# Scaled adjacency stored graph by graph, row of degrees in the raw adjacency's tile, and a new stage order in a two-layer graph network

## The chip, the cores and the metric

The kernel runs on one core of one Trainium2 chip. The time is the device time of one launch in microseconds (us). Several executions are timed and their median is compared; one more execution is profiled, and its span runs from the first to the last instruction. Engines are called TensorE (PE, with PEld for its weight loads), VectorE (DVE), ScalarE (ACT), GpSimd (POOL) and SyncE (SP, which issues nearly all DMAs here).

## The reference

There are 128 graphs of 128 nodes with 512 features each, all in float32, and one adjacency matrix of 128 x 128 per graph.

```
deg = sum(adj, axis=-1)
agg = (adj @ x) / max(deg, 1e-6)
x1  = layernorm(x + relu(concat(x, agg) @ W.T))          # W is 512 x 1024
h1  = relu(adj @ (x1 @ W1) + b1)
h2  = relu(adj @ (h1 @ W2) + b2)
out = layernorm(x1 + adj @ (h2 @ W3) + b3)
```

The kernel uses concat(x, agg) @ W.T = x @ Wa + (adj / deg) @ (x @ Wb), so that the first layer needs x times both halves of W, and then one product per graph with the scaled adjacency.

## The kernel before

**Work units.** The graphs are taken four at a time; the four are called a quad, and there are 32 quads. For each quad the code has 22 named stages: X (load transposed x and build sums of it), D (load the adjacency and compute the degrees), AT (load the transposed adjacency), L0 to L3 (x times both halves of W, called y and u), A0 and A1 (the aggregation: scaled adjacency times y, plus u, then relu, residual and layernorm; two graphs each), G0 to G3 (the products of x1 and the adjacency, one graph each), Ha and Hb (times W1), Sa and Sb (times W2), H2 (times the adjacency), Ta and Tb (times W3), Z0 and Z1 (the last product with the adjacency, layernorm, output).

**Products.** Products with weights use Winograd's form of Strassen's method, so seven block products stand for eight. This needs sums and differences of blocks, on the data (class `Data`) and on the weights (class `Weight`, `sums`, lines 346 to 354). A weight has seven places in its tile. `PLACE` (line 334) says which place each of the seven products reads: product 1 reads place 0, 5 reads 3, 6 reads 2, 2 reads 4, 7 reads 1, 4 reads 5 and 3 reads 6. In quads 0 and 1 the first layer uses one level of the method (line 599 is its matmul). From quad 2 on, most products use two levels (line 617 is the matmul), and the first layer's weights stream in from DRAM through six slots (`ring`, in the trace `ring<-forms` and `big<-forms`), one DMA per block.

**Degrees and scaled adjacency.** For quad q, `load_adj` brings the raw adjacency to the tile `ar`. `degrees` (line 550) reduces it on VectorE to `deg` (line 554), takes the maximum with a small number and the reciprocal (555, 556), writes the 128 x 4 result to DRAM (`dd`) and reads it back as one row of 512 numbers, the same in all 128 partitions, into the tile `ah`. `normalized` (called at the start of stage L0) multiplies the transposed adjacency `at` into `ah` in place. The tile `ah` has the shape [128, 128, 4]: the graph is the innermost index, as it is in the row. In A0 and A1 the matmul at line 916 takes `AH_T[:, :, g]` as its stationary operand. The matmul at line 1216 (Z0 and Z1) has the same shape, with `a[:, g, :]` of the tile `at`, whose shape is [128, 4, 128]. There are one `ar`, one `ah`, two `at`, two `deg` and two `dd`.

**Order.** Nothing is issued directly. The stages append operations, with estimated durations and with the keys that they read and write, to a plan (class `Plan`). The order in which stages advance is the written list `ORDER`: at step t, an entry "L0-3" advances stage L0 of quad t-3, if what `AFTER` asks for is done; otherwise the stage is put on a list and advances as soon as it can. `Plan.order` then simulates the engines with the estimates and picks, for each engine, the next operation. TensorE takes the first ready one of the next `AHEAD` (48) in the order; the other engines take the ready operation with the earliest due time, where due times follow from TensorE's order. `LEADS` are four lead times in us: an operation with a lead isn't started earlier than so long before it is due. The first is that of ScalarE's copies that seed a bank of PSUM, the second that of the loads of x for the residual, the third that of the inner sums, the fourth that of the streamed weights. The emitted program keeps this order on every engine, and SP issues its DMAs in it.

**Start.** The program begins with the loads of x of quad 0 and of the second half of W (`wb`), four blocks each, and with the sums of both. Loads of W1, W2 and W3 wait for the key "row of degrees".

Helpers record most operations, so many instructions bear one line: 327 is every two-operand instruction on VectorE, 329 those on GpSimd, 320 every DMA.

Of the kernel before, what the change touches and what calls it, by code (L numbers as in the profile page):

```python
# [11 lines left out]
OP = mybir.AluOpType  # L12
AX = mybir.AxisListType

P = 128
G = 4
# [19 lines left out]
class Plan:  # L36
# [5 lines left out]


    LAG = 0.15
    AHEAD, HELP, HOLD, SEEN, REST, SPARE = 48, 12.0, 5.0, 8, 25.0, 1
    DMA_US, DMA_RATE = 2.0, 0.22e6

    def __init__(self, pools):
# [176 lines left out]

BANKS = 8
SIZES = 9, 3, 6, 6
LEADS = 9.0, 6.0, 28.9, 943.1
AFTER = {
# [3 lines left out]
}  # L233
ORDER = """
    L2-4 Ta-6 L3-4 Ta-5 Tb-5 Ta-6 Z0-6 L0-3 L3-2 L1-4 Ta-6 Ha-4 L0-3 D L0-3 Sb-3 L1-4 AT-3 L1-3 Tb-6 Sa-4 L1-4 Sa-4
    H2-5 G2-3 L2-4 L2-4 Z0-3 Tb-6 Hb-5 Tb-5 G1-3 H2-5 Tb-6 L0-2 L0-3 Z1-6 X-2 Ha-3 L3-3 L1-3 Z0-5 A0-4 H2-5 G1-4 L3-3
    L3-4 H2-5 L3-3 L3-4 Sb-3 Ha-3 Ha-3 L2-3 Sb-4 Ta-5 Sa-3 G3-4 Tb-5 Tb-5 Sb-3 Hb-4 G2-4 X-1 AT-3 G0-2 Sb-4 L0-2 Ta-5
    A1-3 A1-4 A0-4 G3-4 L0-3 G0-3 H2-4 Sa-4 Sa-3 Z1-5 L1-3 D Sa-4 L0-2 Hb-2 Sa-2 Sb-2 Ha-3 A1-4 Z1-6 L1-3 L2-3 Sa-3
    Tb-5 Ta-5 L3-2 Ha-2 L2-2 L1-2 Sb-2 L2-3 A0-4 Ta-5 Sb-2 L2-3
"""  # L240


# [1 line left out]
def gnn_resnorm_kernel(  # L244
# [15 lines left out]
    nc = tc.nc  # L260
# [13 lines left out]
    def tile_of(shape, name):  # L274
        return sbuf.tile(shape, F32, tag=name, name=name)
# [7 lines left out]
    ROW_T = [tile_of([P, 4, 2, H], f"row{i}") for i in range(2)]  # L283
    U_T = [tile_of([P, 4, 2, H], f"u{i}") for i in range(2)]
    AR_T = tile_of([P, G, P], "ar")
    AT_T = [tile_of([P, G, P], f"at{i}") for i in range(2)]
    AH_T = tile_of([P, P, G], "ah")
    ND = 8
    DEG_T = [tile_of([P, G], f"deg{i}") for i in range(2)]
    DD_T = [dram.tile([P, G], F32, tag=f"dd{i}", name=f"dd{i}") for i in range(2)]  # L290
# [18 lines left out]
    def pinned(ins):  # L309
        return tc.keep_in_program_order(ins)  # L310

    def vector(n, emit, reads, writes, shared=False, lead=None):
        plan.op("DVE", 0.06 + 0.00123 * n, emit, reads, writes, shared, lead=lead)

    def scalar(n, emit, reads, writes, columns=0, lead=None):
        plan.op("ACT", 0.165 + 0.00083 * n + 0.1 * columns, emit, reads, writes, lead=lead)

    def dma(dst, src, reads, writes, size, queue="SP", lead=None):
        eng = nc.sync if queue == "SP" else nc.scalar
        plan.op(queue, 0.06, lambda: pinned(eng.dma_start(dst(), src())), reads, writes, size=size, lead=lead)  # L320

    def const(v):
        return lambda: v

    def add(eng, n, dst, a, b, reads, writes, op=OP.add, shared=False, lead=None):

        on_vector = lambda: pinned(nc.vector.tensor_tensor(dst(), a(), b(), op=op))  # L327
        if eng == "POOL":
            on_gpsimd = lambda: pinned(nc.gpsimd.tensor_tensor(dst(), a(), b(), op=op))  # L329
            plan.op("POOL", 0.03 + 0.00243 * n, on_gpsimd, reads, writes, True, other=(0.06 + 0.00123 * n, on_vector), lead=lead)  # L330
        else:
            vector(n, on_vector, reads, writes, shared)
# [5 lines left out]
    class Weight:  # L338
# [4 lines left out]
        def __init__(self, name, w, after=()):  # L343
            self.name, self.t, self.ti = name, W_T[name], WI_T.get(name)
            wv = w.rearrange("(h c p) (o n) -> p h o c n", p=P, c=2, o=2)
            for i, j, k in ((0, 0, 0), (0, 1, 3), (1, 1, 6), (1, 0, 4)):
                dma(const(self.t[:, k]), const(wv[:, i, j]), after, [(name, k)], P * 2 * H * 4)

        def sums(self):
            for d, a, b in ((1, 6, 3), (3, 3, 0), (2, 6, 3), (5, 4, 2)):  # L350
                add(
                    "DVE", F, const(self.t[:, d]), const(self.t[:, a]), const(self.t[:, b]),
                    [(self.name, a), (self.name, b)], [(self.name, d)], OP.subtract, True,
                )
# [68 lines left out]
    class Streamed:  # L423

        def parts(self, ps, i):
# [3 lines left out]
                lambda: RING_T[s.index][:, 0:n], const(FORMS[i - 1][:, ps[0] : ps[-1] + 1].rearrange("p k s n -> p k (s n)")),  # L429
                ["ring free"] + [("form", w, i, p) for w in range(2) for p in ps], [s], n * P * H * 4, lead=LEADS[3],  # L430
            )
            return [lambda j=j: RING_T[s.index][:, j] for j in range(n)], [s]

    class Data:
# [18 lines left out]
        def inner_sums(self):  # L453
            for ps in PAIRS:
# [13 lines left out]
                for dst, a, b, reads, writes, op in (  # L468
# [4 lines left out]
                ):  # L473
                    add("POOL", n * P, dst, a, b, reads, writes, op, lead=LEADS[2] if dst is first else None)

# [52 lines left out]
    def at(q):  # L528
        return AT_T[q % 2], [("at", q % 2)]

# [12 lines left out]
    def load_adj(q):  # L543
        dma(const(AR_T), const(adj[q]), (), ["ar"], P * F * 4)

# [4 lines left out]
    def degrees(q):  # L550
        d, kd = DEG_T[q % 2], [("deg", q % 2)]
        dd = DD_T[q % 2]
        queue = "ACT" if q == 0 else "SP"
        vector(512, lambda: pinned(nc.vector.tensor_reduce(d, AR_T, axis=AX.X, op=OP.add)), ["ar"], kd)
        vector(90, lambda: pinned(nc.vector.tensor_scalar(d, d, DEG_EPS, None, op0=OP.max)), kd, kd, True)
        vector(90, lambda: pinned(nc.vector.reciprocal(d, d)), kd, kd)
        dma(const(dd), const(d), kd, [("dd", q % 2)], 400000 if q else 800000, queue)
        dma(
            const(AH_T), const(bass.AP(tensor=dd.tensor, offset=dd.offset, ap=[[0, P], [G, P], [1, G]])),
            [("dd", q % 2)], ["ah", "row of degrees"], 400000, queue,  # L560
        )

    def normalized(q):
        t, k = at(q)
        ah = AH_T.rearrange("p i g -> p g i")
        add("DVE", 512, const(ah), const(t), const(ah), k + ["ah"], ["ah"], OP.mult, True)

    def bank_ap(s):
        return BANK[s.index]

    def quarters(p, n):
        return bank_ap(p).rearrange("p a (b n) -> p (a b) n", n=P)[:, 0:n]
# [50 lines left out]
    def v_part(v, n, g, c):  # L623
        return lambda: V_T[v.index][:, 0:n, g, c]
# [56 lines left out]
    def last_part(a, b, ps, joint, v, kv, sinks):  # L681
# [18 lines left out]

        scalar(n * P, lambda: pinned(nc.scalar.copy(quarters(pz, n), v_part(v, n, 1, 1)())), kv, [pz], lead=LEADS[0])
        add("POOL", n * P, v_part(v, n, 0, 1), v_part(v, n, 0, 1), v_part(v, n, 1, 1), kv, [(v, "d")], OP.subtract)
# [120 lines left out]
    def layernorm(i, ap, keys, of=None):  # L823

        i %= ND
        mv, rs = MV_T[i], RS_T[i]
        src, ksrc = of or (ap, keys)
        for j in range(2):
            st = ST_T[(2 * i + j) % ND]
            ks = [("st", (2 * i + j) % ND)]  # L830
            vector(512, lambda j=j, st=st: pinned(nc.vector.bn_stats(st, src(j))), ksrc(j), ks)
            vector(98, lambda j=j, st=st: pinned(nc.vector.bn_aggr(mv[:, j, :], st)), ks, [("mv", i, j)])
        kr, kb = factors(i, range(2))
        for j in range(2):
            r, b = rs[:, 0, j : j + 1], rs[:, 1, j : j + 1]
            scalar(
                512,
                lambda j=j, r=r, b=b: pinned(nc.scalar.activation(ap(j), src(j), AF.Identity, bias=b, scale=r)),
                kr + kb + ksrc(j), keys(j), columns=2,
            )  # L840
# [51 lines left out]
    def l0(q):  # L892
        return row(q, "y"), u_of(q)
# [13 lines left out]
    def seg_agg(q, m):  # L907
        y, u = l0(q)
        for g in (2 * m, 2 * m + 1):
            p, r = Slot("bank", seeded=True), Slot("s", spare=3)  # L910
            dma(lambda r=r: S_T[r.index].rearrange("p a b -> p (a b)"), const(x[q][:, g]), (), [r], P * F * 4, lead=LEADS[1])
            scalar(512, lambda g=g, p=p: pinned(nc.scalar.copy(bank_ap(p), u.graph(g))), u.keys((g,)), [p], lead=LEADS[0])
            plan.op(
                "PE", 0.858,
                lambda g=g, p=p: pinned(
                    nc.tensor.matmul(bank_ap(p), AH_T[:, :, g], y.graph(g), start=False, stop=True, skip_group_check=True)  # L916
                ),
                ["ah"] + y.keys((g,)), [p],
            )
            vector(  # L920
                512,
                lambda g=g, p=p, r=r: pinned(
                    nc.vector.scalar_tensor_tensor(
                        u.graph(g), bank_ap(p), 0.0, S_T[r.index], op0=OP.max, op1=OP.add
                    )
                ),
                [p, r], u.keys((g,)),
            )
            yield
        layernorm(4 * q + m, lambda j: u.graph(2 * m + j), lambda j: u.keys((2 * m + j,)))  # L930
# [194 lines left out]
    def seg_end(q):  # L1125
# [11 lines left out]
        def half(k):  # L1137
            return bank_ap(banks[k])[:, 0]

        for g, h in parts:  # L1140
            p, j = banks[g, h], g - 2
            scalar(
                256, lambda g=g, h=h: pinned(nc.scalar.copy(half((g, h)), u.graph(g)[:, h])), u.keys((g,)), [p], lead=LEADS[0]
            )
# [192 lines left out]
    for t in range(NG + max((lag for _, lag in tokens), default=0)):  # L1337
        for n, lag in tokens:
            q = t - lag
# [57 lines left out]
```

## Time and profile before

| What | Value |
|---|---|
| Median of 3 runs | 2249.04 us (2248.91 to 2249.4) |
| The profiled execution | 2250.41 us |
| Its span | 2248.5 us |
| TensorE matmuls busy | 2235.7 us, 99% of the span, 13624 instructions |
| TensorE weight loads busy | 1997.9 us, 89% |
| VectorE busy | 1534.5 us, 68% |
| ScalarE busy | 1330.8 us, 59% |
| GpSimd busy | 1168.4 us, 52% |
| DMA traffic | 333.14 MB, mean 148 GB/s |
| Granted clock of TensorE | 0.999 |

A line of the groups reads: line, engine, operation, output tile, inputs, shapes, count, then busy time and mean duration of one, then the idle time of that engine just before, with what ended it. Tiles are named without their number. In the timeline neighbouring instructions of one kind are merged, so a row has the start, the length and the count. A float32 matmul appears as two records, each with a weight load of its own. Ends of matmuls are modelled, so neighbouring matmuls overlap in the timeline; the distance from one start to the next is what counts.

### The profile page before, as it was taken

To read this page: it belongs to the slowest core of one execution; us is meant where nothing else is said; L and a number is where in the kernel's file an instruction comes from. 1 tells how busy PE (TensorE), PEld (TensorE's weight loads), DVE (VectorE), ACT (ScalarE), POOL (GpSimd) and SP (SyncE) were. 2 spreads that over 40 slices of the span, in tenths; PEclk is the share of its full clock that TensorE was granted. 3 is DMA by queue.
4 is the path that set the end of the run, shared out by engine and by line. 5 is a ranking of instruction groups with operands and counts; after the bars stand their busy time and mean duration, and the time that the engine had idled before them with its cause. 6 is when DMAs were issued, how large, how long until landed. Compare 5 with 4: busy or idle time off the path is not lost.

```text
span 2248.5 us, 39986 instructions
## 1 busy us (share of the span) xinstructions
PE 2235.7 (99%) x13624; PEld 1997.9 (89%) x13624; DVE 1534.5 (68%) x3384; ACT 1330.8 (59%) x2619; POOL 1168.4 (52%) x1508
## 2 busy tenths in 40 slices
PE   8999999999999999999999999999999999999998
PEld 7888889898898888998888989889898898888997
DVE  4766667666777667677666766667666777667674
ACT  2456656566565665566665656656566556665565
POOL 0245654556645465554565455654546655455540
PEclk9999999999999999999999999999999999999999
DMA  8453445534455444454444553445534455443431
GB/s 268 125 156 125 149 142 174 175 121 145 130 176 176 127 146 134 159 176 140 139 144 143 178 162 124 147 142 172 176 121 149 129 168 176 124 141 129 153 125 38
DMA packets 206330, 333.14 MB, mean 148 GB/s; under 512 B 27056, under 2 KB 72112, under 8 KB 206128
## 3 DMA queue, kind: packets, MB, share of 16 engines
q1 hardware_dynamic: 205696, 330.19, 46.1%
q8 instruction: 109, 1.79, 0.3%
q14 instruction: 93, 0.76, 0.1%
q10 hardware_dynamic: 432, 0.40, 0.1%
HBM read 290.46 MB, written 40.04 MB: 147 GB/s over the span
## 4 chain that ended last, share of the span: by engine, by line
PE 99%; DVE 0%; DMA 0%; issue 0%; SPq 0%; DVEq 0%; ACT 0%
PE bank L617 57%; PE bank L599 21%; PE bank L916 5%; PE bank L941 5%; PE bank L1029 5%; PE bank L1216 5%; DMA big<-in_w0T_dram 0%; DVE big L327 0%; PE bank L1148 0%; SPq L320 0%; DVE ah L327 0%; DVE end_st L1153 0%; DVEq L1392 0%; DVE bank L327 0%; DVE T L327 0%
## 5 line engine op out<-in xcount | busy, mean ns | idle before, releaser
L579 ACT COPY s<-bank 128x384 f32<-128x384 f32 (+1 forms) x567 | 306.6, 541 | 320.6 <-PE bank L617 172.3
L599 PE MATMUL bank<-T,w 128*128 128x256 f32 x1792 | 416.9, 379 | 0.0
L599 PEld LDWEIGHTS bank<-T,w 128*128 128x128 f32 x1792 | 333.5, 190 | 67.2 <-issue 28.7
L329 POOL TENSOR_TENSOR T<-T 128x512 f32<-128x512 f32 (+2 forms) x295 | 279.8, 971 | 199.6 <-DVE T L327 113.2
L327 DVE TENSOR_TENSOR v<-bank,s 128x512 f32<-128x512 f32 x240 | 164.3, 684 | 205.1 <-PE bank L617 204.3
L617 PE MATMUL bank<-big,ti 128*128 128x128 f32 (+1 forms) x1470 | 274.2, 320 | 0.0
L329 POOL TENSOR_TENSOR xT<-xT 128x512 f32<-128x512 f32 (+1 forms) x244 | 237.9, 975 | 36.0 <-DVE ti L327 23.6
L585 ACT COPY bank<-bank 128x512 f32<-128x512 f32 (+2 forms) x273 | 144.0, 527 | 180.0 <-PE bank L617 153.4
L617 PEld LDWEIGHTS bank<-big,ti 128*128 128x128 f32 x1470 | 218.4, 191 | 23.8 <-issue 4.3
L617 PEld LDWEIGHTS bank<-w,T 128*128 128x128 f32 x1680 | 218.3, 192 | 17.1 <-issue 7.2
L327 DVE TENSOR_TENSOR T<-T 128x512 f32<-128x512 f32 (+1 forms) x325 | 223.9, 713 | 8.8 <-ACT T L952 5.8
L617 PEld LDWEIGHTS bank<-w,ti 128*128 128x128 f32 x1680 | 216.1, 192 | 15.5 <-issue 7.2
L617 PE MATMUL bank<-w,T 128*128 128x128 f32 x1680 | 226.5, 275 | 0.0
L617 PE MATMUL bank<-w,ti 128*128 128x128 f32 x1680 | 226.5, 275 | 0.0
L617 PE MATMUL bank<-big,T 128*128 128x128 f32 x1680 | 226.4, 275 | 0.0
L617 PEld LDWEIGHTS bank<-big,T 128*128 128x128 f32 x1680 | 218.3, 192 | 7.7
L327 DVE TENSOR_TENSOR row<-bank,s 128x384 f32<-128x384 f32 (+2 forms) x254 | 119.0, 468 | 152.3 <-PE bank L617 124.8
L617 PE MATMUL bank<-ring,xT 128*128 128x256 f32 x840 | 216.7, 380 | 0.0
L617 PE MATMUL bank<-big,xT 128*128 128x256 f32 x840 | 216.7, 379 | 0.0
L329 POOL TENSOR_TENSOR v<-v 128x384 f32<-128x384 f32 (+1 forms) x61 | 69.3, 1136 | 278.9 <-DVE v L327 144.4
L327 DVE TENSOR_TENSOR v<-v 128x512 f32<-128x512 f32 (+1 forms) x299 | 190.7, 645 | 5.3 <-DVE T L327 0.3
L329 POOL TENSOR_TENSOR s<-s,v 128x256 f32<-128x256 f32 (+1 forms) x60 | 51.8, 863 | 255.2 <-ACT bank L1210 140.7
(99 smaller groups left out, 4166.1 us busy)
## 6 DMA issues: line engine op xcount, KB each, us to landing
big<-forms SPq DMA_DIRECT2D x315, 256.0 KB, 3.2
ring<-forms SPq DMA_DIRECT2D x315, 256.0 KB, 3.3
s<-in_x_dram SPq DMA_DIRECT2D x128, 256.0 KB, 5.9
out_dram<-s SPq DMA_DIRECT2D x126, 256.0 KB, 4.0
xT<-in_xT_dram SPq DMA_DIRECT2D x62, 512.0 KB, 5.6
big<-forms SPq DMA_DIRECT2D x105, 128.0 KB, 2.7
ring<-forms SPq DMA_DIRECT2D x105, 128.0 KB, 2.8
ar<-in_adj_dram SPq DMA_DIRECT2D x32, 256.0 KB, 2.6
```

The costliest lines, as they stand in the source:

```text
L327: on_vector = lambda: pinned(nc.vector.tensor_tensor(dst(), a(), b(), op=op))
L329: on_gpsimd = lambda: pinned(nc.gpsimd.tensor_tensor(dst(), a(), b(), op=op))
L579: scalar(n * P, lambda: pinned(nc.scalar.copy(quarters_of(s, n), quarters(p, n))), [p], [s])
L585: scalar(n * P, lambda: pinned(nc.scalar.copy(quarters(s, n), quarters(p, n))), [p], [s])
L599: nc.tensor.matmul(bank_ap(p)[:, o, :], lhsT, rhs, start=start and o == 0 and c == 0, stop=c == 1, skip_group_check=True,)
L617: nc.tensor.matmul(dst, ta(), tb(), start=start and n == 0, stop=True, skip_group_check=True)
L916: nc.tensor.matmul(bank_ap(p), AH_T[:, :, g], y.graph(g), start=False, stop=True, skip_group_check=True)
L941: nc.tensor.matmul(bank_ap(p)[:, c // 2, (c % 2) * P : (c % 2 + 1) * P], u.chunk(g, c), a[:, g, :], start=c == 0, stop=True, skip_group_ch ...
L1029: nc.tensor.matmul(bank_ap(p)[:, g // 2, (g % 2) * P : (g % 2 + 1) * P], s.chunk(g, o), a[:, g, :], start=g == 0, stop=True, skip_group_ch ...
L1216: nc.tensor.matmul(bank_ap(p), a[:, g, :], s.graph(g), start=False, stop=True, skip_group_check=True)
```

## The change

The row of degrees is read into the tile `ar` and not into `ah`. `normalized` multiplies `at` with that row, which it reads graph by graph with a step of four words, and writes the result to `ah`, which has now the shape [128, 4, 128]. The matmul of the aggregation takes `AH_T[:, g]`. `normalized` now reads the key "ar", so the next load of the adjacency comes after it.

In `Weight`, the raw block b01 is loaded to place 1 in all weights. Place 3 then gets b01 - b00, and place 1 is overwritten with b11 - b01; the seven final contents are the same as before, and so are the numbers of loads and of subtractions.

`AHEAD` goes from 48 to 32, `LEADS` and `ORDER` have new values.

```diff
-    AHEAD, HELP, HOLD, SEEN, REST, SPARE = 48, 12.0, 5.0, 8, 25.0, 1
+    AHEAD, HELP, HOLD, SEEN, REST, SPARE = 32, 12.0, 5.0, 8, 25.0, 1
...
-LEADS = 9.0, 6.0, 28.9, 943.1
+LEADS = 9.9, 5.6, 28.9, 902.9
...
 ORDER = """
-    L2-4 Ta-6 L3-4 Ta-5 Tb-5 Ta-6 Z0-6 L0-3 L3-2 L1-4 Ta-6 Ha-4 L0-3 D L0-3 Sb-3 L1-4 AT-3 L1-3 Tb-6 Sa-4 L1-4 Sa-4
...
+    Sa-4 L0-4 Sb-3 L2-4 Sb-4 Ta-6 L1-3 G2-2 Z1-5 Sa-5 Sb-5 L1-2 Tb-6 D Z1-7 A0-5 L0-2 Sa-5 A0-5 L0-2 Ha-1 G0-4 L2-2
...
+    ROW_OF_DEGREES = AR_T.rearrange("p g i -> p (g i)")
     AT_T = [tile_of([P, G, P], f"at{i}") for i in range(2)]
-    AH_T = tile_of([P, P, G], "ah")
+    AH_T = tile_of([P, G, P], "ah")
...
-            for i, j, k in ((0, 0, 0), (0, 1, 3), (1, 1, 6), (1, 0, 4)):
+            for i, j, k in ((0, 0, 0), (0, 1, 1), (1, 1, 6), (1, 0, 4)):
                 dma(const(self.t[:, k]), const(wv[:, i, j]), after, [(name, k)], P * 2 * H * 4)
 
         def sums(self):
-            for d, a, b in ((1, 6, 3), (3, 3, 0), (2, 6, 3), (5, 4, 2)):
+            for d, a, b in ((3, 1, 0), (1, 6, 1), (2, 6, 3), (5, 4, 2)):
...
         dma(
-            const(AH_T), const(bass.AP(tensor=dd.tensor, offset=dd.offset, ap=[[0, P], [G, P], [1, G]])),
-            [("dd", q % 2)], ["ah", "row of degrees"], 400000, queue,
+            const(ROW_OF_DEGREES), const(bass.AP(tensor=dd.tensor, offset=dd.offset, ap=[[0, P], [1, G * P]])),
+            [("dd", q % 2)], ["ar", "row of degrees"], 400000, queue,
         )
 
     def normalized(q):
         t, k = at(q)
-        ah = AH_T.rearrange("p i g -> p g i")
-        add("DVE", 512, const(ah), const(t), const(ah), k + ["ah"], ["ah"], OP.mult, True)
+        r = ROW_OF_DEGREES.rearrange("p (i g) -> p g i", g=G)
+        add("DVE", 512, const(AH_T), const(t), const(r), k + ["ar"], ["ah"], OP.mult, True)
...
-                    nc.tensor.matmul(bank_ap(p), AH_T[:, :, g], y.graph(g), start=False, stop=True, skip_group_check=True)
+                    nc.tensor.matmul(bank_ap(p), AH_T[:, g], y.graph(g), start=False, stop=True, skip_group_check=True)
```

More of the change, by code (lines that the diff above doesn't have):

```diff
@@ L234 @@
 ORDER = """
-    L2-4 Ta-6 L3-4 Ta-5 Tb-5 Ta-6 Z0-6 L0-3 L3-2 L1-4 Ta-6 Ha-4 L0-3 D L0-3 Sb-3 L1-4 AT-3 L1-3 Tb-6 Sa-4 L1-4 Sa-4
[L236 to L239, printed above, removed]
+    Sa-4 L0-4 Sb-3 L2-4 Sb-4 Ta-6 L1-3 G2-2 Z1-5 Sa-5 Sb-5 L1-2 Tb-6 D Z1-7 A0-5 L0-2 Sa-5 A0-5 L0-2 Ha-1 G0-4 L2-2
+    L0-2 Ta-4 Tb-5 L3 G3-2 Ha-1 L3-3 L0 Sb-1 Tb-5 A0-3 Sb-1 L2-4 Ta-6 Sb-3 Ta-6 L1-4 X Hb-2 Ha-2 L1-2 L3-4 H2-3 A1-4
+    Hb-5 Tb-6 Sa-3 H2-5 L2-3 L2-4 L2-4 Ha Sa-3 D-2 Tb-4 L0-2 Sb-2 A1-1 Sa-1 L1-4 H2-4 Z1-6 Sa-3 L2-2 L3-1 L0-3 L3-1
+    Tb-5 L1-4 L1-4 L3-3 Ha-2 L2-4 L0-3 H2-5 L3-4 Ta-5 L3-4 Hb-3 G0-3 Sa-1 Tb-5 Ta-5 G3-4 G1-2 AT-3 L1-3 AT-2 G1-1 Ta-4
+    Z0-3 Tb-3 A1-4 G2 Ha-1 Z0-4 Ta-5 X H2-3 Sb-2 Z0-1
 """
```

## The prediction

> **What bounds the kernel now.** I read the waits of TensorE first, then the groups of instructions, then TensorE's timeline at the lines that the change touches, then the queue of SP. The waits of TensorE, whole (engine, line, what it waited for: total us, times, longest):
>
> ```profile
> PE bank L599 <- DMA big<-in_w0T_dram: 5.5, 1, 5.5
> PE bank L599 <- DVE T L327: 0.8, 1, 0.8
> PE bank L916 <- DVE ah L327: 0.2, 1, 0.2
> ```
>
> Three waits, 6.5 us of 2248.5, all in the first 90 us. The chain that ended last repeats itself with the quads (start, length):
>
> ```profile
> 755.26 21.75 PE bank L617 x148
> ...
> 824.65 21.75 PE bank L617 x148
> ```
>
> So a quad costs 824.65 - 755.26 = 69.39 us, TensorE never waits in it, and whatever VectorE, ScalarE or a DMA gains there is worth nothing. Only the pace of TensorE's own instructions counts. The groups show one kind that is out of line (busy us, mean ns of one | idle before):
>
> ```profile
> L916 PE MATMUL bank<-row,ah 128*128 128x512 f32 x256 | 128.2, 622 | 0.2 <-DVE ah L327 0.2
> L1216 PE MATMUL bank<-row,at 128*128 128x512 f32 x252 | 123.4, 592 | 0.0
> L916 PEld LDWEIGHTS bank<-row,ah 128*128 128x128 f32 x256 | 74.2, 314 | 15.7 <-DVE ah L327 0.6
> L1216 PEld LDWEIGHTS bank<-row,at 128*128 128x128 f32 x252 | 47.7, 190 | 20.1 <-issue 15.3
> L327 DVE TENSOR_TENSOR ah<-at,ah 128x512 f32<-128x512 f32 x32 | 38.1, 1189 | 39.3 <-DMA at<-in_adjT_dram 39.3
> ```
>
> L916 and L1216 have the same shape and the same moving operand (a graph of a row tile). They differ in the stationary one: `at` is stored graph by graph, 128 neighbouring words per graph; `ah` has the graph innermost, so a graph's weights lie 16 bytes apart. Its weight load takes 314 ns against 190, its matmul 622 ns against 592. The timeline says when that costs TensorE time (start, length; an f32 matmul is two records):
>
> ```profile
> 794.42 1.06 PE L617 MATMUL bank<-big,ti 128*128 128x128 f32 x8
> 795.31 1.14 PE L916 MATMUL bank<-row,ah 128*128 128x512 f32 x2
> 796.29 0.83 PE L617 MATMUL bank<-w,T 128*128 128x128 f32 x6
> ```
>
> The next matmul starts 0.98 us after L916's pair. The first run of L916 in the same quad has three graphs, from 790.83 to 793.53: 2.70 us. A pair of L1216 entered behind a matmul of the same short kind (128 columns) takes 0.86:
>
> ```profile
> 2221.99 1.02 PE L1216 MATMUL bank<-row,at 128*128 128x512 f32 x2
> 2222.85 1.95 PE L1029 MATMUL bank<-at,row 128*128 128x128 f32 x16
> ```
>
> So 0.98 - 0.86 = 0.12 us, and 2.70 - 3 x 0.86 = 0.12 us: it is lost once per run, at its entry, where the matmul in front gives only 0.11 us of cover (8 of them take 0.89 us) for a 0.31 us load. Two runs a quad: 0.24 us of the 69.39.
>
> [...] inside a run the 0.31 us load hides behind a 0.43 us matmul and nothing is lost. [...] The scaling of `ah`, source and destination both at 16-byte steps, takes 1189/512 = 2.3 ns[...]; a contiguous form is in the trace at 713 ns (line 327, T<-T).
>
> **The change part by part.**
>
> *Weights of the aggregation.* `ah` becomes graph by graph, so L916's load is then what L1216's is: 190 ns, and the entry costs nothing. From the groups: (622 - 592) x 256 = 7.7 us; from the quads: 2 x 0.12 x 32 = 7.7 us. **-7.7 us**, on the path. From the other side, if a run entered behind 128 columns still lost a part, down to 0; L1216's pair above, 0.86 with exactly that entry, makes me take the full value.
>
> *The scaling.* 32 instructions, now with one hopping source and a contiguous destination. Between 1189 ns as now and 713 ns[...]. Worth 0: TensorE doesn't wait for it. It starts at 753.62 in the quad above, its first user at 790.83, 36 us after its end; only in the second quad (0.2 us of wait) is that cover gone.
>
> *Row of degrees into `ar`.* Same DMA, 2 KB to each partition, same number. It no longer waits for the aggregation of the quad before to let go of `ah`; it waits for the reduction and the write of the degrees. In return the load of the next adjacency waits until the scaling has read `ar`. Then follow adjacency (2.6 us to land), reduction 0.68, two small ones 0.16 + 0.18, write of the degrees 1.6, row about 3.3: 8.5 us, where the next scaling is 69 us away. Worth 0.
>
> *b01 loaded to its own place.* Four loads and four subtractions per weight as before, so 0 for w1, w2, w3 and the second half of w0, which lie behind TensorE's work. Only the first weight is in the open:
>
> ```profile
> 6.91 2.14 DVE L327 TENSOR_TENSOR big<-big 128x512 f32<-128x512 f32 x3 [6.04 <-DMA big<-in_w0T_dram]
> 8.97 0.42 DVE L327 TENSOR_TENSOR ti<-big 128x256 f32<-128x256 f32 x1
> 9.31 0.68 DVE L327 TENSOR_TENSOR T<-T 128x512 f32<-128x512 f32 x1
> ```
>
> VectorE began when the third block (b11) had landed, since b01 lay where the difference of b01 and b00 must go. Now that difference needs b00 and b01 alone and starts one load earlier, 0.7 us. But TensorE's second product, at 10.05, waits for the sum of T at 9.31, whose last block lands at about 8.9. So at most 0.4 us of the 0.7 come through: **-0.3 us** (between 0 and -0.4; TensorE's first matmuls run at half pace there, 0.43 us instead of 0.22).
>
> *Order, lead times, window of 32.* Instructions on TensorE stay the same in kind and number. Read stage by stage, the new order has the same cycle per quad, with small exchanges among aggregation, second aggregation and layer 3, and the same end for the last quad. What it can still gain is small: the pauses other than those above are about 0.4 us at 86.8 us (the second quad's scaling) and 0.3 us at 2185. Taken as 0, from -0.7; above, no row excludes a loss, which is the second rival.
>
> **Sum.** -7.7 - 0.3 = -8.0 us. Against the profiled execution: span 2248.5 to 2240.5, its time 2250.41 to 2242.4. The median shown is 1.37 us below that execution's time: 2249.04 - 8.0 = **2241.0 us**. A quad goes from 69.39 to 69.15.
>
> **Rivals.** *The entry stall stays.* Should its cause be not the stride but the several waits of L916 (bank seeded by ScalarE, row, `ah`), only the start is gained: 2249.04 - 0.3 = 2248.7. Against it: L1216 waits for a seeded bank too and loses nothing.
>
> *A new wait in each quad, slower.* The three DMAs of the degrees now come right after the scaling, which runs when the streamed weights of the joint product start to flow on the same queue. SP issues in order, so while one of them waits for VectorE, streamed loads stand behind it. Six slots of 4 x 0.216 = 0.86 us each give 5.2 us from release to reuse; a load takes 3.2 to 3.3 us to land; cover 1.9 us. A hold of h costs h - 1.9 each in 30 quads. It eats the gain at h = 1.9 + 8.0/30 = 2.2 us, and is slower by over 0.2% from 2.3 us. At 2.7 us: 2241 + 24 = 2265. For it: the queue has had longer holds (total, times, longest):
>
> ```profile
> SPq L320 <- PE bank L916: 117.1, 36, 6.4
> SPq L320 <- DVE deg L554: 100.0, 28, 3.9
> SPq L320 <- DMA ah<-dd: 80.4, 28, 3.5
> ```
>
> Against it: these are the very waits that the change removes or shortens (row behind L916, adjacency behind the reduction, write behind the row's landing), and none reached TensorE. The new one, behind the scaling, is planned at 0.69 us[...].
>
> *Part of the gain lost.* Seeding banks 0.9 us earlier holds banks longer; a pause of 0.1 to 0.2 us per quad would give 2244 to 2247.
>
> **Chances.** Forecast 0.80; part lost 0.07, half of it still past the limit; entry stall stays 0.05; slower 0.08. A difference of 0.2%, 4.5 us, is about what can be told from none. Faster 0.83, same 0.09, slower 0.08. The forecast's own range is 2239 to 2243.5 (start and order at their best, or some 2 us of scattered pauses); the range for 8 in 10 reaches into the partial loss: 2238.5 to 2246.5.
>
> **What would show it.** Right: L916's load at 190 ns and matmul at 592; pairs of L916 0.86 us apart at each entry; a quad of 69.15 us; no wait of TensorE beyond the start; the scaling below 1.1 us; SP no longer waiting for DVE deg L554. Wrong: a wait of TensorE for streamed loads, banks or `ah` in every quad, or the entry still at 0.98.

## The result: 0.35% slower

The changed kernel takes 2258.27 us (median of 7 runs, 2254.73 to 2260.54), the kernel before 2249.29 us on the same chip: ratio 1.0035, 95% interval 1.0026 to 1.0044. The prediction was 2241.0 us, faster. The profiled execution has a span of 2256.4 us against 2248.5.

The aggregation did what was forecast. From the groups of the changed kernel (line numbers are one higher than before; busy us, mean ns of one | idle before):

```profile
L917 PE MATMUL bank<-row,ah 128*128 128x512 f32 x256 | 125.4, 593 | 0.0
L917 PEld LDWEIGHTS bank<-row,ah 128*128 128x128 f32 x256 | 41.5, 191 | 16.5 <-ACT bank L913 9.6 <-issue 6.7
L328 DVE TENSOR_TENSOR ah<-at,ar 128x512 f32<-128x512 f32 x32 | 35.8, 1119 | 3.2 <-DMA at<-in_adjT_dram 3.2
```

The weight load went from 314 to 191 ns, the matmul from 622 to 593. The scaling is hardly faster, 1119 ns after 1189. But TensorE's waits have two new lines, for streamed weights:

```profile
PE bank L600 <- DMA big<-in_w0T_dram: 5.1, 1, 5.1
PE bank L618 <- DMA ring<-forms: 3.1, 4, 1.0
PE bank L618 <- DMA big<-forms: 2.4, 2, 1.6
```

The chain that ended last shows one of them (start, length):

```profile
1521.58 22.07 PE bank L618 x146
...
1591.17 22.08 PE bank L618 x146
...
1620.63 5.25 DMA ring<-forms
...
1661.91 22.08 PE bank L618 x146
```

The first of these two quads takes 69.59 us, the one with the DMA on the chain 70.74; before it was 69.39, predicted 69.15. So there is a loss in every quad, and a larger one in some. The first kind is not in the list of waits. It shows in the timeline of TensorE, at the matmuls of stage H2 (L1030), and beside them VectorE's:

```profile
1543.49 1.05 PE L1030 MATMUL bank<-at,row 128*128 128x128 f32 x8
1544.38 0.83 PE L618 MATMUL bank<-w,ti 128*128 128x128 f32 x6
1545.06 2.94 PE L1030 MATMUL bank<-at,row 128*128 128x128 f32 x24
1547.83 0.38 PE L618 MATMUL bank<-big,ti 128*128 128x256 f32 x1
```

```profile
1545.33 0.56 DVE L328 TENSOR_TENSOR row<-bank,s 128x384 f32<-128x384 f32 x1 [1.56 <-PE bank L618]
```

Eight records take 0.89 us from start to start, so 24 should take 2.67; they take 2.77. The product `w,ti` begins at 1544.38, VectorE sums its result into the row from 1545.33 to 1545.89, and the second of the three H2 groups, due at 1545.95, reads that row. There is one group of 0.89 us between, and the way over VectorE takes a little longer.

To count all such losses I took the distance between the starts of neighbouring matmuls, less the usual one of their kind (0.112 us for 128 columns, 0.216 for 256, 0.429 for 512), wherever more than 0.015 us was left. "Pauses" below means this, between 130 and 2150 us of the span, so in the steady part:

| Pauses, us | before | after |
|---|---|---|
| Entry of the aggregation | 7.0 | 0 |
| Streamed joint products, over 0.15 us each | 0 | 6.7 |
| Streamed joint products, up to 0.15 us each | 0.0 | 7.4 |
| H2 (L1030) | 0 | 2.7 |
| Z (L1217) | 0 | 1.6 |
| Sum | 7.0 | 18.3 |

The steady part lost 11.3 us. Before 130 us the pauses and half-pace matmuls fell from 5.7 to 2.1, after 2150 us they rose by 0.4. Together +8.1 us, and the span grew by 7.9.

### The profile page after: what moved, and what is told of

Its sections match the earlier page's. It is cut to its first block, busy times and chain, and to the rows that moved or that the text cites. A ratio compares the mean times of both kernels' runs of the same rounds, so it can differ in the third digit from the quotient of the medians.

```text
span 2256.4 us, 39844 instructions
## 1 busy us (share of the span) xinstructions
PE 2238.9 (99%) x13624; PEld 1963.4 (87%) x13624; DVE 1524.8 (68%) x3376; ACT 1331.4 (59%) x2619; POOL 1227.9 (54%) x1516
## 3 DMA queue, kind: packets, MB, share of 16 engines
q8 instruction: 109, 1.79, 0.3%
## 4 chain that ended last, share of the span: by engine, by line
PE 98%; DMA 1%; ACT 0%; DVE 0%; issue 0%; DVEq 0%; SPq 0%; ACTq 0%
PE bank L618 56%; PE bank L600 22%; PE bank L1030 5%; PE bank L942 5%; PE bank L917 5%; PE bank L1217 5%; DMA ring<-forms 1%; DMA big<-forms 0%; DMA big<-in_w0T_dram 0%; PE bank L1149 0%; DVE end_st L1154 0%; DVEq L1393 0%; ACT u L839 0%; ACT T L953 0%; ACT bank L586 0%
## 5 line engine op out<-in xcount | busy, mean ns | idle before, releaser
L580 ACT COPY s<-bank 128x384 f32<-128x384 f32 (+1 forms) x567 | 304.6, 537 | 291.8 <-PE bank L618 200.7
L600 PE MATMUL bank<-T,w 128*128 128x256 f32 x1792 | 407.3, 379 | 0.0
L330 POOL TENSOR_TENSOR T<-T 128x512 f32<-128x512 f32 (+1 forms) x243 | 231.8, 969 | 171.3 <-PE bank L600 59.8
L618 PE MATMUL bank<-big,ti 128*128 128x128 f32 (+1 forms) x1512 | 282.3, 321 | 0.0
L328 DVE TENSOR_TENSOR T<-T 128x512 f32<-128x512 f32 (+1 forms) x377 | 215.2, 591 | 70.9 <-ACT T L966 38.9
L618 PEld LDWEIGHTS bank<-big,ti 128*128 128x128 f32 x1512 | 227.2, 191 | 28.2 <-issue 14.9
L328 DVE TENSOR_TENSOR v<-v 128x512 f32<-128x512 f32 (+1 forms) x301 | 222.4, 747 | 1.4 <-DVE rstd L328 0.4
L618 PE MATMUL bank<-ring,xT 128*128 128x256 f32 x852 | 222.2, 383 | 0.0
L1227 DVE SCALAR_TENSOR_TENSOR s<-bank,u 128x512 f32<-128x512 f32 x124 | 85.4, 689 | 201.8 <-PE bank L1217 201.7
L330 POOL TENSOR_TENSOR ti<-T 128x256 f32<-128x256 f32 (+1 forms) x149 | 90.7, 617 | 197.9 <-DVE ti L328 197.9
```

What stands on the lines that cost most here:

```text
L580: scalar(n * P, lambda: pinned(nc.scalar.copy(quarters_of(s, n), quarters(p, n))), [p], [s])
L600: nc.tensor.matmul(bank_ap(p)[:, o, :], lhsT, rhs, start=start and o == 0 and c == 0, stop=c == 1, skip_group_check=True,)
L618: nc.tensor.matmul(dst, ta(), tb(), start=start and n == 0, stop=True, skip_group_check=True)
L1227: nc.vector.scalar_tensor_tensor(S_T[o.index], bank_ap(p), 1.0, u.graph(g), op0=OP.mult, op1=OP.add, accum_out=total)
```

## The experiments

The ratios are against the kernel before, timed beside each run (medians of 2249.29 to 2251.23 us), so a difference between the medians of two experiments is uncertain by 1 or 2 us.

**The layout alone.** The order of all engines is that of the kernel before:

```diff
-    AH_T = tile_of([P, P, G], "ah")
+    AH_T = tile_of([P, G, P], "ah")
+    ROW_OF_DEGREES = tile_of([P, G, P], "rowd").rearrange("p g i -> p (g i)")
...
-        ah = AH_T.rearrange("p i g -> p g i")
-        add("DVE", 512, const(ah), const(t), const(ah), k + ["ah"], ["ah"], OP.mult, True)
+        r = ROW_OF_DEGREES.rearrange("p (i g) -> p g i", g=G)
+        add("DVE", 512, const(AH_T), const(t), const(r), k + ["ah"], ["ah"], OP.mult, True)
...
```

> The kernel before, with the order of every engine untouched; only the scaled adjacency is stored graph by graph, and the row of degrees is read into a tile of its own, from which the scaling reads it. Theory (the layout takes the entry stall of the aggregation away, and it is the new order that lost time): L916's weight load 190 ns, no 0.12 us at the entry of its runs, a quad of 69.15 us, 2249.3 - 7.7 = 2241.6 us. Rival (the layout itself brings a wait elsewhere, through the slower or earlier scaling): 2249 us or more.

Measured: 2243.46 us, ratio 0.997 (0.9959 to 0.9982). TensorE's waits are those of the kernel before, and the chain gives a quad of 820.00 - 750.86 = 69.14 us:

```profile
PE bank L599 <- DMA big<-in_w0T_dram: 5.5, 1, 5.5
PE bank L599 <- DVE T L327: 1.0, 1, 1.0
PE bank L916 <- DVE ah L327: 0.2, 1, 0.2
```

```profile
750.86 21.75 PE bank L617 x148
...
820.00 21.75 PE bank L617 x148
```

Pauses in the steady part fell from 7.0 to 0.4 us. The layout wins 0.3%, as forecast; the loss comes from elsewhere.

**The order without the layout.** The changed kernel with the old storage of `ah`:

```diff
-    AH_T = tile_of([P, G, P], "ah")
+    AH_T = tile_of([P, P, G], "ah")
...
-        add("DVE", 512, const(AH_T), const(t), const(r), k + ["ar"], ["ah"], OP.mult, True)
+        add("DVE", 512, const(AH_T.rearrange("p i g -> p g i")), const(t), const(r), k + ["ar"], ["ah"], OP.mult, True)
...
```

> The changed kernel, with the order of every engine untouched; only the scaled adjacency has the graph as its innermost index again. Theory (layout and order are independent, the order costs some 16 us and the layout wins 7.7): 2258 + 7.7 = 2266 us, the entry stall of 0.12 us back in each run of the aggregation. Rival (with the other waits there, the entry stall is hidden behind them): 2258 us as the changed kernel.

Measured: 2268.80 us, ratio 1.0085 (1.0071 to 1.0099). That is 10.5 us above the changed kernel (11 by the ratios), not 7.7. The pauses at the entry of the aggregation are back with 10.6 us in 87 events, three in a quad where the kernel before had two: the new order splits the four matmuls into three runs. The entry stall is there with either order, and without the new layout the rest of the change costs 0.85%.

**b01 at its own place, alone.** The two lines of `Weight` in the kernel before:

```diff
-            for i, j, k in ((0, 0, 0), (0, 1, 3), (1, 1, 6), (1, 0, 4)):
+            for i, j, k in ((0, 0, 0), (0, 1, 1), (1, 1, 6), (1, 0, 4)):
...
-            for d, a, b in ((1, 6, 3), (3, 3, 0), (2, 6, 3), (5, 4, 2)):
+            for d, a, b in ((3, 1, 0), (1, 6, 1), (2, 6, 3), (5, 4, 2)):
```

> The kernel before, with b01 loaded to its own place and the sums in the new sequence, and the old order list (the planned order differs a little, mostly in the first quads). Theory: the start gains what the two profiles differ by in the first product of TensorE, up to 3 us of pauses and half-pace matmuls, so 2246.5 to 2249 us. Rival (the start gains nothing, since its pace was set by the landing of x and by when TensorE reaches full pace): 2249 us.

Measured: 2247.71 us, ratio 0.9988 (0.9981 to 0.9994), so 2.7 us. VectorE's timeline at the start shows why it is more than the 0.3 of the prediction:

```profile
6.44 0.69 DVE L327 TENSOR_TENSOR T<-T 128x512 f32<-128x512 f32 x1 [5.57 <-DMA T<-in_xT_dram]
7.66 2.09 DVE L327 TENSOR_TENSOR big<-big 128x512 f32<-128x512 f32 x2 [0.53 <-DMA big<-in_w0T_dram]
```

The sum of T, before at 9.31, stands now in front. Since the second product no longer needs b11, the planner gives that load a later due time and issues x first. TensorE's second product starts at 9.07 us and not at 10.05. The rest lies in the half-pace matmuls: their 33rd starts at 14.36 us and not at 17.23. How much of that is luck can't be told from single profiles, since the layout alone, with the start of the kernel before, has it at 15.36.

**Both data parts, old order list.** The edits of the first and the third experiment together.

> The kernel before with its old order list, the scaled adjacency graph by graph with the row of degrees in a tile of its own, and b01 loaded to its own place: both parts of the change that touch data, without the new order, the new lead times and the window of 32. Theory (the three parts add up): 7.7 us from the layout and 2.7 from the start, 2250.4 - 10.4 = 2240 us, faster than both kernels; so the new order alone costs some 18 us. Rival (the parts overlap at the start, or the order of before has no room either): 2243 us as the layout alone.

Measured: 2240.54 us, ratio 0.9953 (0.994 to 0.9967): the parts add up, and this is faster than both kernels. Steady pauses are 1.2 us. What the changed kernel has besides (the shared tile, the order, the lead times, the window) therefore costs 1.0035 / 0.9953 = 1.0082, some 18 us. No run takes the order list, the lead times and the window apart.

**The x loads made small.** The changed kernel with

```diff
-dma(lambda r=r: S_T[r.index].rearrange("p a b -> p (a b)"), const(x[q][:, g]), ...
+dma(lambda r=r: S_T[r.index].rearrange("p a b -> p (a b)")[:, 0 : 512 if q < 4 else 64], const(x[q][:, g, 0 : 512 if q < 4 else 64]), ...
```

> The changed kernel, with the order of every engine untouched; from quad 4 on the loads of x for the residual carry 64 of the 512 features (the other 448 columns of the residual are left out, the slot keeps what it held). The same number of DMAs stands in the queue. Theory (the streamed weights come late because the burst of x loads shares the DMA engines with them): no wait of TensorE for streamed loads, the 6.7 us of pauses over 0.15 us in the middle gone, 2258 - 7 = 2251 us; small pauses of 0.05 to 0.09 us stay where they are not at streamed loads. Rival (SP holds them back, or their slots come free too late): 2258 us, the waits unchanged.

Measured: 2252.89 us, ratio 1.0012 (1.0005 to 1.0018), 5.4 us below the changed kernel. TensorE's waits for streamed weights fell from 5.5 us to 0.9:

```profile
PE bank L618 <- DVE u L328: 0.8, 1, 0.8
PE bank L618 <- DMA ring<-forms: 0.7, 1, 0.7
PE bank L600 <- DVE big L328: 0.2, 1, 0.2
PE bank L618 <- DMA big<-forms: 0.2, 1, 0.2
```

Pauses over 0.15 us fell from 6.7 to 2.4; the small ones hardly moved (6.5 at joint products, 2.6 at H2, 1.6 at Z). The burst is in SP's timeline of the changed kernel, around the load that stood on the chain:

```profile
1618.04 0.32 SPq L321 DMA_DIRECT2D ring<-forms  x1
1618.47 1.66 SPq L321 DMA_DIRECT2D big<-forms  x3
1620.63 0.32 SPq L321 DMA_DIRECT2D ring<-forms  x1
1621.00 0.90 SPq L321 DMA_DIRECT2D s<-in_x_dram  x2
1621.94 0.90 SPq L321 DMA_DIRECT2D ring<-forms  x2
```

The landing times grow within this burst, from 2.06 us for its first load to 8.00 for its last x load, issued at 1623.85. The streamed load issued at 1620.63 took 5.25 us to land, where the median is 3.5.

To see how much time a load has in hand, each one was matched with the product that reads its place, by the slots of the plan. The last six streamed loads of a quad land 1.2 to 3.6 us before their use in the kernel before (medians by place), and 0.2 to 1.25 us before it in the changed one, 0.13 at the least, as with the load on the chain: it landed at 1625.89 and TensorE, which waited for it, began at 1626.02. The kernel before has a burst of the same kind, but it comes later in the quad:

```profile
784.06 0.32 SPq L320 DMA_DIRECT2D big<-forms  x1
784.50 0.36 SPq L320 DMA_DIRECT2D ring<-forms  x1
784.91 0.90 SPq L320 DMA_DIRECT2D s<-in_x_dram  x2
```

The load of 784.50 is the last one of its quad. In every steady quad the first x load is issued 0.4 us or more after that last one, and the next six streamed loads, which share its burst, have 12 us and more in hand. In the changed kernel the first x load of the aggregation is issued 0.9 us or more before the last streamed one, in every steady quad. With small x loads that last load lands in 3.6 us instead of 5.4 (medians).

**A seventh place for streamed weights.** The changed kernel; the plan still knows six slots, but a load goes to the place that has been free for the longest:

```diff
-    RING_T += [tile_of([P, 2, H], f"ring{i}") for i in range(NR - 3)]
+    RING_T += [tile_of([P, 2, H], f"ring{i}") for i in range(NR - 2)]; FREE = list(range(NR + 1))
...
+            def place():
+                s.at = FREE.pop(0)
+                return RING_T[s.at][:, 0:n]
+
+            def used(j):
+                if j == n - 1:
+                    FREE.append(s.at)
+                return RING_T[s.at][:, j]
...
```

> The changed kernel, with the order of every engine untouched; only the streamed weights go round in seven places in memory instead of six, so that a load needn't wait for the latest release. Theory (the last loads of a quad are issued as late as their place allows, and then meet the burst of x loads): their reserve grows by up to 0.9 us, the pauses over 0.15 us go, 2258 - 7 = 2251 us. Rival (bandwidth alone decides, whatever the issue): 2256 to 2258 us.

Measured: 2251.08 us, ratio 1.0001 (0.9993 to 1.0009). No wait of TensorE for a streamed load is left:

```profile
PE bank L610 <- DMA big<-in_w0T_dram: 5.1, 1, 5.1
PE bank L610 <- DVE big L328: 0.2, 1, 0.2
```

Pauses over 0.15 us in the steady part are gone. So the late loads have two causes that must meet: the release of a place sets when they are issued, and the x loads then stretch their landing. Taking either away is enough for most of the 7 us (5.4 us with small x loads, 7.2 with seven places).

**A tile of its own for the row, new order.** The changed kernel with

```diff
-    ROW_OF_DEGREES = AR_T.rearrange("p g i -> p (g i)")
+    ROW_OF_DEGREES = tile_of([P, G, P], "rowd").rearrange("p g i -> p (g i)")
```

> The changed kernel, with the order of every engine untouched; only the row of degrees is read into a tile of its own, so the next adjacency needn't wait for the scaling to read the row. Rival of the prediction (SP, held behind the scaling, delays streamed weights): SP's 18.7 us of waits for the scaling gone and 2258 falls to 2251 us or less. Theory (these holds fall where streamed loads have over 5 us in hand): 2258 us, with TensorE's waits as they are.

Measured: 2259.63 us, ratio 1.0038 (1.0025 to 1.005), no different from the changed kernel. In the changed kernel SP waits like this (total, times, longest):

```profile
SPq L321 <- DMA dd<-deg: 54.1, 30, 3.9
SPq L321 <- DVE deg L557: 37.4, 29, 9.3
SPq L321 <- DVE ah L328: 18.7, 27, 6.1
```

The last of these lines is gone in this run, and the steady pauses are 18.7 us as against 18.3. SP's wait for the scaling cost nothing.

**One product moved.** The kernel with seven places, and in 30 quads the joint product that follows the four H2 groups moved ahead of the third of them, on TensorE alone:

```diff
...
+    for late in [o for o in order if getattr(o, "h2", None) == 3]:
+        pe = [o for o in order if o.engine == "PE"]
+        i = pe.index(late)
+        if [getattr(o, "h2", None) for o in pe[i - 1 : i + 2]] == [0, 3, 1]:
+            first, at_ = pe[i + 2], order.index(late)
...
+                order.remove(first)
+                order.insert(at_, first)
...
```

> The kernel of the run before (the changed kernel with seven places for streamed weights); in 30 quads one joint product of 0.43 us is moved ahead of the third H2 matmul group on TensorE, so that VectorE's sum of the rows that this group reads has 0.43 us more. All other engines keep their order. Theory (the pauses of 0.09 us are round trips TensorE, VectorE, TensorE for which the order leaves too little other work): the 29 pauses at L1030, 2.7 us in all, go: 2251.1 - 2.7 = 2248.4 us. Rival (the pause belongs to the entry of this kind of matmul, like the strided entry before): they stay, 2251 us.

Measured: 2249.29 us, ratio 0.9995 (0.9988 to 1.0001), after 1.0001. The pauses at H2 went from 2.7 us to none:

```profile
1540.95 0.60 PE L628 MATMUL bank<-ring,ti 128*128 128x256 f32 x2
1541.38 1.95 PE L1040 MATMUL bank<-at,row 128*128 128x128 f32 x16
1543.17 0.60 PE L628 MATMUL bank<-ring,xT 128*128 128x256 f32 x2
```

Sixteen records now take 1.79 us, twice the 0.89 of eight. Some 0.8 us came back as new small pauses at the joint products, whose own spacing was disturbed, so the steady sum fell from 10.0 to 8.4. The intervals of the two runs overlap, so the gain in time isn't shown; the disappearance of the pauses is.

The small pauses at the joint products and at Z look the same. The plan says what each product needs, and the trace of the changed kernel says when that was done. Of the 7.4 us at joint products, 5.6 lie where a copy by ScalarE out of the product's bank (L580) had ended 0.10 us before the product began, and 1.6 where a streamed load had landed some 0.14 us before it. At Z it is VectorE's sum into the row, 0.06 to 0.11 us before. One of the copies, with the product behind it:

```profile
1553.21 0.59 ACT L580 COPY s<-bank 128x512 f32<-128x512 f32 x1 [0.49 <-PE bank L618]
1553.90 1.08 PE L618 MATMUL bank<-big,xT 128*128 128x256 f32 x4
1554.82 0.59 PE L618 MATMUL bank<-ring,xT 128*128 128x256 f32 x2
```

The four records take 0.92 us from start to start where 0.86 is usual. In the kernel before, these copies and sums end at least 0.34 us before the product that needs them. Only the pauses at H2 were taken away by an experiment; for the others this is read from the times.

**The old list with the shared tile.** The changed kernel with `ORDER`, `LEADS` and `AHEAD` of before.

> The changed kernel with the order list, lead times and window of the kernel before. Reading the row into the adjacency's tile changes what a DMA waits for, so the planner takes other decisions from the same list. Theory (the old list fits the old waits only; the search for a new one was needed because of the shared tile): waits of TensorE in many quads, well over 2258 us, by the planner's own estimate some 110 us more. Rival (the old list does as well here as it does with a tile of the row's own): 2240 us.

Measured: 2310.56 us, ratio 1.0265 (1.0235 to 1.0295). TensorE now waits for all kinds of things:

```profile
PE bank L618 <- ACT bank L702: 6.1, 19, 0.4
PE bank L618 <- ACT bank L586: 5.8, 9, 0.6
PE bank L618 <- POOL T L330: 5.5, 9, 0.6
```

Steady pauses are 67.9 us. With a tile of the row's own and the old waits in the plan the same list gives 2240.54 us. So it is with the shared tile that the old list fails, and the new order isn't as good as the old one was without it. Against the kernel before the loss is 59 us on the chip, half of the planner's estimate.

## Why the prediction was wrong

*Weights of the aggregation, -7.7 us: right.* The layout alone gave a ratio of 0.997, 6.8 us, a quad of 69.14 us where 69.15 was forecast, and pauses of 0.4 us instead of 7.0. The weight load follows the step of 16 bytes: 191 ns in that run after 314, and 317 with the old storage in the new order. By what mechanism was not shown. Not foreseen: the gain depends on how many runs the order makes, 10.6 us in the new one.

*The scaling, worth 0: right,* though its duration was not. The forecast had it below 1.1 us; it measured 1119 ns. What is left of the step of four words is one source, and that the destination's step cost anything isn't shown: the run with the old storage in the new order, where both have it, took 1125 ns, and the layout alone, where the source has it, 1157. The lower bound of 713 ns was misread: it is the mean of two shapes, and the 235 instructions with 512 columns in that group take 845 ns.

*Row of degrees into `ar`, worth 0: right for the waits, wrong for what follows.* With a tile of its own the changed kernel is no faster. But the step asked only whether the moved transfers would be late. It left out that the plan is made anew from the changed waits; the old list then gives 2310.56 us.

*b01, -0.3 us: too small.* It measured 2.7. The step took the landing order of the first loads as given; the planner changed it.

*Order, lead times, window, taken as 0: this is the step that failed.* It compared the sequence of the stages, found it alike, and concluded that the new order would again have no waits. The sequence is alike, but the kernel before lived on reserves that the stage list doesn't show: 1.2 to 3.6 us in hand for the last streamed loads, x loads that come only after them, and at least 0.34 us between the copies and sums named above and the product that needs them. The new order leaves 0.2 to 1.25 us for these loads, and 0.06 to 0.11 us at some five hand-overs of the other kind in each quad. It costs some 18 us, by the ratio of the run with both data parts; 18.3 us of pauses are found in its steady part, against 1.2 in that run.

*The rival "a new wait in each quad, slower"* named the right victim, the streamed weights, the right outcome, and a cover of 1.9 us that lies within what the kernel before had. Its mechanism was wrong: SP held behind the scaling cost nothing. It also reckoned with a landing of 3.2 to 3.3 us, the median; in the burst the load on the chain took 5.25. And it took every streamed load for four matmul records; of the 28 loads of a quad, 21 bring two blocks (256 KB, four records) and seven bring one (128 KB, two), so the loads are not one per block, as the description of the kernel has it. That the cover came out near the true one is in part luck. Of the 18 us, this place makes 6.7 in pauses over 0.15 us; the rival got a chance of 0.08.

The planner doesn't see this loss. Its own simulation, run without the chip, ends at 2233.8 us for the kernel before and at 2235.0 for the changed one. In it an operation may start as soon as what it needs is ready, so an operand with 0.1 us in hand counts as much as one with 3 us. What stays open is which of the three, the list, the lead times or the window, brings the loss, and by experiment also the cause of the small pauses at the joint products and at Z.

## What to carry to other kernels

A kernel whose bound engine hardly waits has little to gain from a new order and much to lose: look at the reserve of each hand-over (landing to use, result to next reader), not at the sequence, before you call a new order neutral. Where an order was fitted to a set of waits, change the data layout in a way that keeps these waits, here with 2 KB more per partition for a tile, and the gain of the layout comes whole. The list of waits missed pauses of up to 0.1 us; the distance from start to start of the bound engine's instructions shows them, and in the changed kernel they were more than half of the loss.

## What the runs showed of the hardware

In the kernel before, a weight load at a step of 16 bytes took 314 ns, where one of neighbouring words took 190. It cost TensorE time only where a short matmul was in front of it: 0.12 us behind 128 columns, nothing inside a run of 512 columns.

How close a hand-over may be: in the steady part of the changed kernel TensorE paused at all 160 products for which the last thing they needed from another engine or a DMA was done 0.04 to 0.14 us before their start, and at one of those for which it was done 0.15 us before or earlier. A sum of 0.56 us on VectorE between two products of TensorE wasn't hidden by 0.89 us of other work (a pause of 0.09 us remained), and was by 0.89 + 0.43 us.

The pace of TensorE's first matmuls, one in 0.43 us, lasted until 13.8 us in the profile of the kernel before and until about 10.4 in that of the layout alone, which has the same start. That is 8.3 and 4.9 us after the first matmul. In the changed kernel it lasted until about 9.2 us, 4.1 us after the first matmul. The clock granted meanwhile was 1.00 in the profiles of both kernels (from 5 to 14 us before, from 5 to 9 after). Why the pace is half at first, and what ends it, no run here tested.
